# The last layers of a four-layer hybrid network: list-schedule order, and layer norm factors brought to the rows by DMA

## The chip, the cores and the metric

The kernel runs on one core of a Trainium2 chip. The metric is device time in microseconds (us), taken as the median of several runs. A core has five engines with queues of their own: TensorE (PE; its weight loads are listed as PEld), VectorE (DVE), ScalarE (ACT), GpSimd (POOL) and SyncE (SP), which issues the transfers here. Products are written to PSUM, which has eight banks of 2 KB per partition; 512 fp32 columns fill one bank.

## The reference, cut to what matters

Four images of 96 channels and 64x64 pixels pass through four layers. Layers 0 and 1 are state-space scans (Mamba, and a scan in four directions). The change concerns layers 2 and 3, which see each image as 4096 tokens of 96 channels:

```python
t = _to_tokens(x)
t = t + _L2_attn_ref(_ln_t(t), ...)   # spectral: 96->192, BN, ReLU, FFT over 4096 tokens, complex
                                      # diagonal + ReLU, inverse FFT, 192->96, BN
t = t + _L2_ffn_ref(_ln_t(t), ...)    # 96->384->96, operands rounded to fp8e5, sums to fp16
t = t + _L3_attn_ref(_ln_t(t), ...)   # linear attention without softmax, 6 heads of 16
t = t + _L3_ffn_ref(_ln_t(t), ...)    # as the first feed-forward

def _ln_t(v, eps=1e-5):
    m = jnp.mean(v, axis=-1, keepdims=True)
    s = jnp.var(v, axis=-1, keepdims=True)
    return (v - m) / jnp.sqrt(s + eps)
```

There are thus four layer norms over the channels per image: one for the spectral layer, three for the rest. The tokens lie on the free axis and the channels on the partitions, so the mean and the variance of a token are sums over partitions.

## The kernel before

`stage_mamba` and `stage_ss2d` compute layers 0 and 1, and `stage_tokens` computes layers 2 and 3 from the buffer `mid2` in DRAM. The first two stages record every operation in a `Plan`: each operation gets an engine, a modelled cost, its predecessors and, for PSUM tiles of the tag `mm`, a `Hold` on a buffer that is chosen late. `Plan.order` then plays a list schedule over five engine clocks: each engine takes the ready operation with the lowest index, and an operation that finds no free buffer is parked. `Plan.run` issues the operations in that order (in the profile they all stand at L467).

`stage_tokens` is written without the planner: its instructions are issued in the order of the Python code. It works in blocks of W = 512 tokens, eight per image. Two generators run in each round of the loop over images: `spectral(t)` for image b, and the chain `ffn`, `attention`, `ffn` for image b-1 (the rest stream). After each `yield` the loop takes the next step from the stream that has done the smaller share of its steps (`SPECTRAL, REST = 100, 170`). So there are five rounds: image 0's spectral layer alone, three rounds with both streams, and the rest stream of image 3 alone. Inside a stream, `lanes` interleaves two or three blocks with a skew. The spectral stream has four PSUM banks (`pa`), the rest stream three (`pb`), and one more (`pv`) sums the attention's key-value products.

The layer norm (`layer_norm_steps`) does for one block of 512 tokens:

- one product with `center_w` (identity minus 1/96), which gives the centred tokens `ln_cent` in PSUM (L524);
- two passes of ACT: the square to `ln_sq` (L527), and a copy to `d` in SBUF (L528), which is `ln_d` or the output itself;
- four products with `ln_sq` as weights and the column `mean_w` as the moving operand, one column each, which put the variances of 512 tokens into a 128x4 tile `ln_var` (L532);
- `rsqrt`: an add on DVE (L507) and a power on POOL (L509), which give `ln_rs`, 128x4;
- four products (L544) of `ln_rs`, broadcast to 96 columns, with the identity: they bring the factors back to the rows, `ln_rstd`, 96x512 in PSUM;
- one multiply on DVE, `d` times `ln_rstd` (L551 to fp8, L553 to fp32).

The spectral layer computes the 4096-point transform as 64 x 64: `h_ps` (96 to 192 channels, L1442), `fa_ps` (first transform of 64, L1455, two tiles of one bank each, copied out by DVE and ACT), `x_ps` (twiddled second transform, L1470) with `u` on ACT and `z` on DVE, `zw_ps` (L1490), `bz_ps` (L1508) and `o_ps` (L1522). The feed-forward uses `f_ps` (L1539 and L1548) with fp8 operands, with `fy` and `fo` as fp16 steps between and `hq` cast on POOL. The attention uses `kv_ps`, `vk_ps` and `at_ps`. The tile `t` holds an image; there are two, so that image b is loaded once image b-2 has been stored.

## Time and profile before

| | |
|---|---|
| median of 3 runs | 7759.35 us (7758.62 to 7760.86) |
| profiled execution: time | 7736.41 us |
| profiled execution: span of the core | 7734.3 us |
| mean granted TensorE clock | 0.906 |
| PE busy | 6714.1 us (87%) |
| DVE busy | 5775.7 us (75%) |
| POOL busy | 5765.4 us (75%) |
| ACT busy | 4616.8 us (60%) |

The profile is that of one execution, whose own time stands beside its span. Busy time of PE contains records that overlap, since products are pipelined; the granted clock is the share of full speed that the hardware allowed TensorE. In the rows of groups a line number names the place in the kernel, then come engine, operation, output and inputs, shapes, count, busy time and mean duration of one, and the engine's idle time just before, with what ended it. An fp32 product shows as two records.

### The profile page before, as it was taken

What the parts mean: (1) busy time and instruction counts of PE and PEld (TensorE: products, weight loads), DVE (VectorE), ACT (ScalarE), POOL (GpSimd) and SP (SyncE); (2) the same over time, 40 slices, a digit from 0 to 9 for tenths busy, and PEclk for the clock granted to TensorE, in tenths of its full rate; (3) what the DMA queues carried; (4) which work ended last, traced back from release to release, by engine and by line L of the source; (5) the groups of instructions that cost most, each with busy time, mean ns of one, the idle gap of its engine ahead of it and who ended that gap; (6) DMA issues with size and microseconds to landing.
All of it is one profiled execution on the core that took longest, in us unless ns stands there. A gap on an engine that the chain in (4) does not pass through costs nothing.

```text
span 7734.3 us, 84473 instructions
## 1 busy us (share of the span) xinstructions
PE 6714.1 (87%) x28872; PEld 2880.5 (37%) x28872; DVE 5775.7 (75%) x4491; ACT 4616.8 (60%) x6903; POOL 5765.4 (75%) x2836
## 2 busy tenths in 40 slices
PE   7988889888988877879898898889898877999997
PEld 2322233223323222223232322223232226888784
DVE  5989988988898882888888877788888873344343
ACT  4655555555555544767777766677777654445442
POOL 5989988989899882889898978789898971222323
PEclk9999999999999988889999897899899878889897
DMA  6988888988888874888888977788887862000000
GB/s 172 235 231 230 230 212 225 246 221 221 225 230 226 225 190 130 216 214 214 208 217 208 237 185 205 205 205 206 207 211 209 219 170 64 2 17 2 17 9 9
DMA packets 473180, 1374.15 MB, mean 178 GB/s; under 512 B 105678, under 2 KB 123807, under 8 KB 470700
## 3 DMA queue, kind: packets, MB, share of 16 engines
q1 hardware_dynamic: 472748, 1368.76, 68.5%
q8 instruction: 227, 3.72, 0.2%
q14 instruction: 205, 1.68, 0.1%
HBM read 1188.18 MB, written 180.36 MB: 177 GB/s over the span
## 4 chain that ended last, share of the span: by engine, by line
PE 53%; DVE 23%; issue 7%; ACT 6%; POOL 6%; DMA 5%; SPq 0%; DVEq 0%; POOLq 0%; ACTq 0%
PE mm L467 18%; PE s L467 14%; DVE sc_d L467 10%; DVE s L467 6%; PE y L467 5%; DVE sc_u L467 4%; POOL sc_h L467 3%; PE x_ps L1470 2%; DMA sc_d<-dd 2%; PE ln_rstd L544 2%; PE ln_cent L524 2%; PE ln_var L532 2%; PE zw_ps L1490 1%; DVE ysum L467 1%; PE h_ps L1442 1%
## 5 line engine op out<-in xcount | busy, mean ns | idle before, releaser
L467 POOL TENSOR_TENSOR sc_h<-sc_d,bc 128x1024 f32<-128x1024 f32 x1024 | 2407.0, 2357 | 375.5 <-DVE sc_d L467 255.9
L467 DVE TENSOR_TENSOR_SCAN sc_d<-sc_d,carry,s 128x1024 f32<-128x1024 f32 x768 | 1801.2, 2346 | 57.5 <-ACT sc_d L467 7.5
L467 DVE TENSOR_TENSOR s<-s,bc 128x1024 f32<-128x1024 f32 x1024 | 1249.3, 1220 | 503.7 <-PE s L467 339.5
L467 PE MATMUL s<-du,c_sel 96*128 96x512 f32 x2048 | 1170.7, 706 | 245.5 <-DVE sc_d L467 200.3
L467 ACT ACTIVATE sc_d<-sc_d,w_alog 128x1024 f32<-128x1024 f32 x1024 | 1166.8, 1146 | 308.5 <-DMA sc_d<-dd 304.7
L467 POOL TENSOR_TENSOR sc_u<-sc_u,bc 128x1024 f32<-128x1024 f32 x512 | 1207.1, 2358 | 191.8 <-ACT bc L467 117.1
L467 POOL TENSOR_TENSOR sc_h<-sc_u,bc 128x1024 f32<-128x1024 f32 x512 | 1207.2, 2358 | 118.0 <-PE y L467 100.7
L467 PE MATMUL y<-sc_h,c_red 128*32 128x512 f32 x6144 | 1072.4, 650 | 79.1 <-POOL sc_h L467 72.7
L467 DVE TENSOR_TENSOR_SCAN sc_u<-s,carry,sc_u 128x1024 f32<-128x1024 f32 x384 | 895.4, 2332 | 55.3 <-ACT s L467 38.9
L467 PE MATMUL s<-du,c_selp 128*128 128x512 f32 x1408 | 730.6, 648 | 112.4 <-DVE sc_d L467 109.3
L467 PEld LDWEIGHTS s<-du,c_sel 96*128 96x128 f32 x2048 | 419.4, 219 | 915.3 <-issue 464.6
L467 ACT ACTIVATE s<-sc_d,w_alog 128x1024 f32<-128x1024 f32 x512 | 570.6, 1115 | 193.5 <-DVE sc_d L467 117.7
L467 ACT ACT_TABLE_LOAD x492 | 631.2, 1283 | 12.9 <-DMA sc_d<-dd 4.3
L467 DVE TENSOR_TENSOR_SCAN sc_d<-sc_d,s 128x1024 f32<-128x1024 f32 x256 | 583.1, 2283 | 17.7 <-ACT sc_d L467 2.9
L509 POOL TENSOR_TENSOR ln_rs<-ln_rs_e,mhalf 128x4 f32<-128x4 f32 x128 | 134.5, 1052 | 566.7 <-DVE ln_rs_e L507 565.1
L467 PE MATMUL mm<-xp,w_conv 96*96 96x512 f32 x1152 | 523.0, 600 | 4.9 <-ACT bc L467 1.9
L467 PEld LDWEIGHTS y<-sc_h,c_red 128*32 128x32 f32 x6144 | 191.3, 113 | 790.9 <-issue 508.0
L467 PEld LDWEIGHTS s<-du,c_selp 128*128 128x128 f32 x1408 | 262.4, 201 | 540.4 <-issue 269.8
L467 ACT COPY carry<-sc_d 128x1 f32<-128x1 f32 x768 | 142.9, 186 | 478.7 <-DVE sc_d L467 470.2
L467 ACT COPY bc<-mm 128x512 f32<-128x512 f32 x512 | 282.8, 581 | 204.6 <-PE mm L467 199.9
L467 PE MATMUL mm<-hn,conv_w 97*64 97x512 f32 (+1 forms) x1024 | 368.3, 615 | 19.9 <-DVE hn L467 19.8
L467 DVE TENSOR_TENSOR_SCAN sc_u<-s,sc_u 128x1024 f32<-128x1024 f32 x128 | 290.7, 2271 | 25.2 <-ACT s L467 22.4
(211 smaller groups left out, 9436.0 us busy)
## 6 DMA issues: line engine op xcount, KB each, us to landing
sc_d<-dd SPq DMA_DIRECT2D x1536, 512.0 KB
sc_u<-ud SPq DMA_DIRECT2D x512, 512.0 KB
dd<-delta SPq DMA_DIRECT2D x128, 448.0 KB
bc<-bcd SPq DMA_DIRECT2D x64, 512.0 KB
ud<-du SPq DMA_DIRECT2D x192, 128.0 KB
dd<-delta SPq DMA_DIRECT2D x32, 512.0 KB
ud<-du SPq DMA_DIRECT2D x32, 512.0 KB
x<-x0d SPq DMA_DIRECT2D x64, 192.0 KB
```

Source lines behind the costliest of these rows:

```text
L467: getattr(getattr(self.nc, op.engine), method)(*a, **kw)
L509: nc.gpsimd.tensor_tensor(rs, ve, self.mhalf[:p, 0:n], ALU.pow)
L524: nc.tensor.matmul(mps, self.center_w, x[:, cs], start=True, stop=True)
L532: nc.tensor.matmul(vps[:, j:j + 1], sq[:, j * 128:(j + 1) * 128], self.mean_w, start=True, stop=True)
L544: nc.tensor.matmul(rps[:, j * 128:(j + 1) * 128], rs[:, q:q + 1].to_broadcast([128, C]), self.ident, start=True, stop=True,)
L1442: nc.tensor.matmul(ph[q * 64:(q + 1) * 64, j, :], xv[:, g * 4 + j, :], w1t[:, q * C:(q + 1) * C], start=True, stop=True,)
L1470: nc.tensor.matmul(px[:, j, :], fa[q][:, :, g * 4 + j], twid[:, g * 4 + j, :], start=True, stop=True)
L1490: nc.tensor.matmul(pw[:, j, :], zs[q][:, j, :], w2[:, q, :], start=q == 0, stop=q == 1)
```

## The change

`stage_tokens` records its work in a `Plan` too. The order is then the planner's over all images at once; the two streams still decide the index of each operation, with steps weighted by what they hold. Five further edits go with it.

- **The norm.** A local function `norm` replaces `layer_norm_steps` in this stage. The centred tokens stay in PSUM (tag `ln`, four banks) and are read there by the last multiply; the copy to `d` goes. The variance products take every fourth token as weights, so that token 4t+q lands in row t, column q, and run against `mean_w` broadcast to 64 columns; one of the 64 is read. The 128x4 factors are written to a line of 512 numbers in DRAM, and read back to 96 partitions by a second transfer (`rows`); the four products with the identity go.
- **PSUM.** All products share three banks (`mm`), with four for `ln` and one for `vk`.
- **Loads.** Image 0 is loaded before the weights; the weights of the feed-forward use the space of `fa` and are loaded at once instead of by turns through the `kv` buffers; the twiddle table comes in eight pieces.
- **Memory.** The two `xl` tiles with their row of ones are made once; `fo` shares the two buffers of `fy`, and `o` those of `u`.
- **The planner.** An operation may take several buffers of a ring at once (the two `fa_ps` tiles), a freed buffer wakes all parked operations, a product's form includes its type, and `side_by_side` takes the cost of each further product. These also apply to the first two stages, which use the same class.

The loops of `h_ps` and `fa_ps` are the same before and after; each group of products is now one operation of the planner.

```diff
@@ Plan
-            op.form = out.ap[0][1], a[1].ap[0][1]
+            op.form = out.ap[0][1], a[1].ap[0][1], a[2].dtype
...
             if new:
-                assert len(new) == 1
+                assert len({id(h.ring) for h in new}) == 1
                 buffers, parked = free[id(new[0].ring)]
-                if not buffers:
-                    heappush(parked, (op.index, op))
+                if len(buffers) < len(new):
+                    parked.append(op)
                     continue
-                since = min(b[0] for b in buffers)
+                buffers.sort(key=lambda b: b[0])
+                since = buffers[len(new) - 1][0]
...
-                    if parked:
-                        _, o = heappop(parked)
+                    for o in parked:
                         heappush(wait[o.engine], (end, o.index, o))
+                    parked.clear()
@@ stage_tokens
-    nc, tc = k.nc, k.tc
-    k.loose = True
+    tc = k.tc
+    pl = Plan(k.nc, least=180.0)
...
-    pa = ctx.enter_context(tc.tile_pool(name="t_pa", bufs=4, space=PSUM))
-    pb = ctx.enter_context(tc.tile_pool(name="t_pb", bufs=3, space=PSUM))
-    pv = ctx.enter_context(tc.tile_pool(name="t_pv", bufs=1, space=PSUM))
+    dr = pl.pool(ctx.enter_context(tc.tile_pool(name="t_dr", bufs=1, space=DRAM)), 4)
+    ps = pl.pool(
+        ctx.enter_context(tc.tile_pool(name="t_ps", bufs=1, space=PSUM)), 3, {"mm": [128, W], "ln": [C, W]}
+    )
+    nc = k.nc = pl
...
+    ts = [load_image(0)]
...
+    def norm(x, out):
+        cent = ps.tile([C, W], F32, tag="ln", name="ln_cent", bufs=4)
+        nc.tensor.matmul(cent, k.center_w, x, start=True, stop=True)
+        sq = wk.tile([C, W], F32, tag="ln_sq", name="ln_sq", bufs=2)
+        nc.scalar.activation(sq, cent, AF.Square)
+        var = ps.tile([128, 4, 64], F32, tag="mm", name="ln_var")
+        cols = sq.rearrange("p (t q) -> p q t", q=4)
+        with nc.side_by_side(overlap=280.0):
+            for q in range(4):
+                nc.tensor.matmul(
+                    var[:, q, :], cols[:, q, :], k.mean_w.to_broadcast([C, 64]), start=True, stop=True
+                )
+        rs = k.rsqrt(wk, var[:, :, 0], EPS, "ln_rs")
+        rd = dr.tile([1, W], F32, tag="ln_rd", name="ln_rd")
+        nc.sync.dma_start(out=rd.rearrange("o (t q) -> (o t) q", q=4), in_=rs)
+        rows = wk.tile([C, W], F32, tag="ln_rows", name="ln_rows", bufs=3)
+        nc.sync.dma_start(out=rows, in_=bass.AP(rd.tensor, rd.offset, [(0, C), (1, W)]))
+        if out.dtype == F8:
+            nc.vector.tensor_tensor(out, cent, rows, ALU.mult, saturate=False)
+        else:
+            nc.vector.tensor_tensor(out, cent, rows, ALU.mult)
...
-            streams.append((spectral(t), SPECTRAL))
+            if b > 0:
+                ts.append(load_image(b))
+            streams.append((spectral(ts[b], xls[0]), spectral_steps))
...
-            done[n] += 1
-            if next(streams[n][0], streams) is streams:
+            weight = next(streams[n][0], 0)
+            done[n] += weight
+            if not weight:
                 live.remove(n)
+    pl.run(tc)
+    k.nc = pl.nc
```

The planner counts 2.2 us plus a term for the bytes for a transfer (about 3.0 us for `rows`), and for the products the cost of the first plus the given `overlap` for each further one.

## The prediction

> **What bounds the kernel now.** I read the page's slices first, to see where the changed stage lies.

> ```profile
> PE   7988889888988877879898898889898877999997
> POOL 5989988989899882889898978789898971222323
> PEclk9999999999999988889999897899899878889897
> ```

> Each digit is a tenth of busy time in 193 us. Up to slice 33 DVE, POOL and the DMA share the load; from there POOL falls to 2 or 3 and PE stands at 9. That tail, 6411 to 7735 us or 1324 us, is stage_tokens. The earlier stages keep their code, so the answer lies in the tail. Next, the windows over its five rounds: length, then busy us of PE, PEld, DVE, ACT and POOL with instruction counts, granted clock, DMA share, GB/s.

> ```profile
> 6436.00:6468.00 32.00, 26.37 (x144) 18.16 (x144) 6.48 (x16) 8.53 (x16) 8.05 (x8) 0.87 0.29 71
> 6468.00:6620.00 152.00, 139.61 (x2050) 137.00 (x2050) 59.10 (x91) 75.42 (x122) 3.51 (x1) 0.90 0.01 2
> 7220.00:7520.00 300.00, 291.27 (x2868) 243.60 (x2868) 115.02 (x237) 145.36 (x258) 84.59 (x97) 0.93 0.04 12
> 7520.00:7735.00 215.00, 167.20 (x676) 103.20 (x676) 63.59 (x133) 64.09 (x120) 72.02 (x89) 0.74 0.03 9
> ```

> Image 0's norms take 32 us and its spectral layer, alone, 152 us. Then come three rounds of 300 us with both streams, PE 97% busy. The last round holds the rest stream alone: PE 78% busy at clock 0.74. No other engine is above 50%, so TensorE bounds the stage: its work, its clock, and its waits at the seams. Third, the groups (busy us, mean ns; idle before). An fp32 product is two records.

> ```profile
> L544 PE MATMUL ln_rstd<-c_ident,ln_rs 128*96 128x128 f32 x1024 | 173.7, 320 | 34.4 <-POOL ln_rs L509 34.4
> L524 PE MATMUL ln_cent<-t,c_center 96*96 96x512 f32 x256 | 158.6, 707 | 24.6 <-DMA t<-mid 20.3 <-DVE t L1528 4.3
> L532 PE MATMUL ln_var<-c_mean,ln_sq 96*128 96x1 f32 x1024 | 139.4, 257 | 13.6 <-ACT ln_d L528 9.4 <-ACT ln_sq L527 4.1
> L1522 PE MATMUL o_ps<-c_twid,bz 128*96 128x64 f32 x512 | 87.6, 342 | 0.7 <-ACT bz L1513 0.7
> ```

> The 128 layer norms (8 + 24 per image) take 472 us of PE busy time. Records overlap, so the true price is start to start, from the timeline: a full-clock stretch of a mixed round, then the last round.

> ```profile
> 7126.11 0.98 PE L532 MATMUL ln_var<-c_mean,ln_sq 96*128 96x1 f32 x8
> 7126.94 2.90 PE L1470 MATMUL x_ps<-c_twid,fa 128*96 128x128 f32 x16
> ...
> 7131.44 1.04 PE L544 MATMUL ln_rstd<-c_ident,ln_rs 128*96 128x128 f32 x8
> 7132.32 2.83 PE L1470 MATMUL x_ps<-c_twid,fa 128*96 128x128 f32 x16
> ...
> 7135.20 1.02 PE L524 MATMUL ln_cent<-t,c_center 96*96 96x512 f32 x2
> 7136.06 0.38 PE L1539 MATMUL f_ps<-xq,f 96*128 96x512 fp8e5 x1
> ```

> ```profile
> 7565.26 2.02 PE L544 MATMUL ln_rstd<-c_ident,ln_rs 128*96 128x128 f32 x8 [0.46 <-POOL ln_rs L509]
> 7567.07 1.06 PE L1548 MATMUL f_ps<-hq,f 128*96 128x512 fp8e5 x2
> ...
> 7574.02 2.02 PE L544 MATMUL ln_rstd<-c_ident,ln_rs 128*96 128x128 f32 x8 [0.71 <-POOL ln_rs L509]
> ```

> At full clock a norm costs PE 0.83 us (variance), 0.88 (rstd) and 0.86 (centring); in the last round rstd alone costs 1.81 plus a 0.46 us wait, in a block of 8.76 us. Last, the chain across the stage's start (start, us).

> ```profile
> 6402.65 2.68 DMA szt<-szd
> 6417.26 5.10 DMA f_in<-in_w_f_dram
> 6425.42 10.87 DMA t<-mid
> 6436.29 1.99 PE ln_cent L524 x2
> ```

> The image is loaded behind all the weights, and PE waits for it until 6436.

> **The change, part by part.** *rstd products.* Removed: 512 products. In a mixed round 32 norms x 0.88 = 28 us at full clock (by busy time 40; the rest is overlap). In the last round, 16 feed-forward norms x (1.81 + 0.46) = 36, and 8 attention norms, at clock near 1, x 0.88 = 7.

> *Variances in 64 columns, from strided weights.* Not in the trace. Lower bound: the single-column price, 0.83. Upper: o_ps, also 64 columns with strided weights, eight records in 2.52 / 2 = 1.26 us (16 records in 2.52 us in the chain). I take the middle, 1.05, since the old one is already paced by weight loading: +0.22 x 32 = 7 us a round (0 to 14), some 8 in the last round at its lower clock (0 to 20).

> *Factors through DRAM.* Added per norm: a write of 2 KB, then a read of 192 KB to 96 partitions. The read has a row, szt<-szd, 2.68 us. For the write the nearest rows are SP's waits for bcd<-bc_part, 196.2 us in 105 waits, longest 5.8; I take 2.7 (2 to 5.8). Norm latency: 0.86 + 0.60 (square) + 1.05 + 0.16 + 1.05 (pow) + 2.7 + 2.68 + 0.68 (multiply) + 8 handoffs of 0.1 = 10.6 us, all with the centred tokens in PSUM. Four such banks give one norm per 2.65 us: 85 us for the 32 norms of a round, under its 300; 64 for the last round's 24, under its 215. I cost it at nothing there: x_ps, zw_ps and the others cover it in mixed rounds. Without cover it shows where norms come in a row ahead of other work, at the start (below). On DVE the multiply now waits for a DMA, and z, fy and the fa copies are queued behind it. The planner counts 2.2 and 3.0 us for the two transfers, so it is placed in time if these hold; a write of 5.8 would be 3 us late, 96 us a round out of the 185 that DVE idles. On SP, 256 more issues of 0.43 us, 110 us in 1324, with a wait of 2.7 us before each read; image loads and stores queue behind it, but SP now waits 1276 us for POOL at L1555.

> The trace has PE at clock 0.67 in 10 us windows of the last round although PE is 85% busy there, and at 1.00 in windows as busy with x_ps. [...]

> *ACT and POOL.* 128 copies to ln_d or xl go (0.577 us each, 74 us of ACT), and with them 9.4 us of PE waits; six of eight memsets (3.5 us) leave POOL. Off the path otherwise.

> *List order and banks.* Seven PSUM banks for products (four spectral, three rest) become three shared ones, plus four for centred tokens. Gains: rounds are no longer walled off, so work fills seams such as 7216 to 7246, at clock 0.50 to 0.82. Full-clock PE work of a mixed round now: spectral 140 (152 less waits in fa), norms 32 x 2.57 = 82, feed-forward 96 products x 0.22 = 21, attention 27 (kv, vk and at, 123.6 / 4 less overlap): 270, against 300 measured; 24 of the 30 are the clock (0.92), the rest waits. After: 270 - 28 + 7 = 249. I keep 27 of the 30: seams fill, three banks add waits. Round 276, minus 24; three rounds, minus 72.

> *Last round.* -43 + 8, and list order recovers 10 of PE's 48 idle us: minus 45. The next limits are lower: POOL per block 1.05 + 3 x 0.61 + 1.16 = 4.1 us; the two fy buffers, now also holding fo, 3.9 us; PE 6.5.

> *Start.* The image is issued first. All of 6.2 MB at the 312 GB/s seen there take 20 us from 6413; the factors queue behind c_twid, so the first multiply comes near 6437, the last four norms a bank turn (10.6) later, h near 6450 instead of 6468: minus 15 (0 to -25). Image 0's own 152 us stay.

> *Earlier stages.* The planner wakes all parked steps instead of one and adds the type to a form. Their only bf16 product has 48 rows, a form of its own already. Zero, bounds 10 either way.

> *What is nothing.* The loops of the first transform (fa) stand in the same order as before; its two tiles are taken together.

> Sum: -72 - 45 - 15 = -132 us on the profiled execution's 7736.4, so 7604. The median, 7759.35, is 23 above that execution; I carry that over: **7627 us**.

> **Rivals.** *A, the waits at the seams go as well.* Mixed rounds at 249 + 12 = 261 (minus 39 each), the last one at full clock, minus 75, start -20: -212, 7547. For it: x_ps stretches already run at 1.00. Against: norms alone do not.

> *B, three banks take back the gain of the mixed rounds.* Losses of 50 instead of 27 give 299; 60 are left from start and end: 7700.

> *C, three banks make it slower.* Per round some 230 tiles pass through them. Product plus evacuation: x_ps 32 x 3.2 = 102, zw 41, h 34, fa 43, bz 21, o 27, f 74, kv 20, at 13, var 39: 414 us, and 46 for two handoffs each: 460. In a 276 us round three banks offer 828, 56% used. The place: fa takes two banks at once, while single-bank steps grab each one that comes free, and ACT and DVE, half busy, keep tiles waiting. It decides once holds exceed 2.1 times these sums (980 / 3 = 327 us a round eats the other 60 and 16 more); at 2.3 times, 353 us a round: +153 - 60, 7852. For it: the old streams had seven banks. Against: in 6510 to 6580 x_ps and zw_ps kept PE 99% busy on four banks with no other stream.

> *D, no change,* where losses near 70 a round just cancel it: 7759.

> **How the numbers follow.** Chances: forecast 0.55, A 0.12, B 0.13, C 0.15, D 0.05. A measurement of this kernel can tell 0.2%, 15.5 us, from no change. Forecast, A and B are faster: 0.80; D same: 0.05; C slower: 0.15. The forecast's own range is 7575 to 7695, from the start (15), variances (40), the last round (25), early stages (10) and 15 us of loss per round, not all at once. The whole range, 7540 to 7770, leaves out C and the lower part of A.

> **What would show it.** Right: no L544 rows in the tail; PE busy in the tail down by 100 to 150 us; var rows between 140 and 215 us; mixed rounds of 270 to 285 us, the last near 170; h_ps starting 15 us earlier after the weights. Wrong: waits of PE for ACT or DVE to free mm tiles above 30 us a round (B, C); waits for DMA rows ahead of xq or h_ps, and a last round that stays above 200; or stages before 6411 that move by more than 10 us.

## The result, and the profile after

The changed kernel takes 7781.19 us (median of 16 runs, 7764.6 to 7813.15), the kernel before 7759.67 us (16 runs). The ratio is 1.003, with an interval of 1.0018 to 1.0042. It is slower by 21.5 us, where 7627 us and a gain were predicted, and the time lies above the range (7540 to 7770).

The profiled execution after took 7785.78 us, its span is 7783.6 us. Against the profile of before that is 49 us more, of which 20 lie ahead of the changed stage. The last addition of the scan stage ended at 6434.0 us (before: 6413.8); among all the kernels below it ended anywhere from 6399 to 6445 us. I therefore compare the tail from that moment on: 1320.5 us before, 1349.7 after, 29 more. These are single executions: planner_only, whose last stage is that of before, has a tail of 1333.8 us, so some 13 us of the 29 can be chance, most of it in the start. First, the same lines of the page as before:

```profile
PE   7988888888988877889898888889898877999997
POOL 5989989988898972889898969689898871221313
PEclk9999999999999988889898898889898877789786
```

PE is as busy in the tail as before, but the granted clock in the last seven slices fell from 8889897 to 7789786. Next, the windows by round of the kernel after: length, then busy us of PE, PEld, DVE, ACT and POOL with counts, granted clock, DMA share and GB/s. A round ends with the last addition of an image's spectral output; the first line holds image 0's norms and its spectral layer.

```profile
6434.00:6656.80 222.80, 178.96 (x2152) 165.40 (x2152) 73.44 (x123) 82.69 (x136) 14.66 (x13) 0.76 0.18 49
6656.80:6959.10 302.30, 295.93 (x2587) 238.12 (x2587) 115.64 (x225) 126.20 (x218) 71.01 (x85) 0.84 0.12 26
6959.10:7270.20 311.10, 305.37 (x2614) 242.72 (x2613) 124.65 (x238) 130.52 (x227) 80.32 (x96) 0.82 0.14 32
7270.20:7581.20 311.00, 304.02 (x2606) 242.25 (x2606) 125.39 (x238) 128.93 (x224) 79.16 (x95) 0.82 0.13 29
7581.20:7783.60 202.40, 158.39 (x499) 95.47 (x497) 71.46 (x142) 57.64 (x105) 79.96 (x98) 0.67 0.16 36
```

In a mixed round PE has 250 to 280 matmuls fewer than before, and yet it is busy 296 to 305 us instead of 289 to 295. So in these rounds PE does not wait more; its instructions take longer. The same cuts for the kernels that matter below (us, with the granted clock in brackets; one profiled execution each):

| kernel | start and image 0 | mixed 1 | mixed 2 | mixed 3 | last | tail |
|---|---|---|---|---|---|---|
| before | 206.9 (0.85) | 295.4 (0.92) | 303.7 (0.92) | 300.4 (0.93) | 214.1 (0.74) | 1320.5 |
| planner_only | 215.0 (0.79) | 295.9 (0.93) | 305.1 (0.91) | 303.8 (0.92) | 214.1 (0.74) | 1333.8 |
| after | 222.9 (0.76) | 302.3 (0.84) | 311.2 (0.82) | 310.9 (0.82) | 202.4 (0.67) | 1349.7 |
| contig_weights | 214.8 (0.79) | 278.0 (0.88) | 301.3 (0.80) | 293.6 (0.83) | 199.0 (0.65) | 1286.7 |
| no_round_trip | 190.7 (0.84) | 299.2 (0.83) | 307.7 (0.83) | 307.2 (0.83) | 182.2 (0.69) | 1287.0 |
| wide_strided | 215.0 (0.82) | 293.9 (0.91) | 306.9 (0.88) | 305.9 (0.86) | 204.4 (0.71) | 1326.2 |
| before_wide | 205.9 (0.86) | 285.0 (0.97) | 291.6 (0.96) | 290.9 (0.96) | 206.0 (0.84) | 1279.4 |
| wide_contig | 208.2 (0.85) | 268.6 (0.91) | 272.8 (0.94) | 280.1 (0.92) | 197.4 (0.73) | 1227.1 |
| list_old_norm | 190.7 (0.89) | 285.2 (0.92) | 286.8 (0.94) | 282.3 (0.96) | 167.1 (0.84) | 1212.1 |
| wide_old_norm | 189.1 (0.90) | 276.3 (0.98) | 281.1 (0.98) | 280.7 (0.99) | 153.1 (0.91) | 1180.3 |
| wide_no_round_trip | 182.1 (0.90) | 254.3 (0.97) | 263.1 (0.97) | 259.0 (1.00) | 169.3 (0.80) | 1127.8 |

before and planner_only run the same last stage: their rounds agree within 3.4 us, but for the start, which differs by 8.

**The variance products.** The groups of the kernel after in the tail, the variances and the centring (busy us, mean ns; idle before):

```profile
L472 PE MATMUL mm<-c_mean,ln_sq 96*128 96x64 f32 x1024 | 256.8, 413 | 31.0 <-ACT ln_sq L472 30.5 <-ACT fa L472 0.4
L472 PE MATMUL ln<-t,c_center 96*96 96x512 f32 x256 | 193.5, 854 | 31.9 <-DVE xl L472 18.7 <-DMA t<-mid 11.0 <-DVE t L472 2.1
```

The variances are busy 256.8 us instead of 139.4, and a record lasts 413 ns instead of 257. Start to start, from the timeline of a stretch where the clock still stood at 1.00:

```profile
6869.01 1.02 PE L472 MATMUL ln<-t,c_center 96*96 96x512 f32 x2
6869.87 1.43 PE L472 MATMUL mm<-c_twid,fa 128*96 128x128 f32 x8
6871.14 1.98 PE L472 MATMUL mm<-c_mean,ln_sq 96*128 96x64 f32 x8
6872.95 1.99 PE L472 MATMUL mm<-w_w,z 96*128 96x96 f32 x16
```

The centring still takes 0.86 us, the variances of one norm 1.81 (6871.14 to 6872.95) instead of 0.83. That is 0.98 us more, and the products with the identity that went away had cost 0.88. Over the whole tail it is the same: the 57 norms whose variances ran at full clock (0.98 or more) and had no wait behind them have a median of 1.85 us (before: 0.81 of 89). On PE the change is thus a loss before anything else counts.

**The start.** The timeline of PE after the image has come:

```profile
6452.55 3.87 PE L472 MATMUL mm<-c_mean,ln_sq 96*128 96x64 f32 x16
6473.37 3.73 PE L472 MATMUL ln<-t,c_center 96*96 96x512 f32 x4 [16.95 <-DVE xl L472]
6476.89 3.79 PE L472 MATMUL mm<-c_mean,ln_sq 96*128 96x64 f32 x16
...
6495.48 4.77 PE L472 MATMUL mm<-w1t,xl 97*64 97x96 f32 x58 [7.74 <-DVE xl L472]
```

After four norms the four banks of centred tokens are full, and PE waits 17 us for the first multiply, then 7.7 us for the last ones; `h_ps` (the last line) begins 61 us after the scan stage's end, where it was 54 before. The timeline of SP and DVE shows what the multiply waited for:

```profile
6458.71 1.62 SPq L472 DMA_DIRECT2D ln_rd<-ln_rs  x2
6469.64 0.79 SPq L472 DMA_DIRECT2D ln_rows<-ln_rd  x2
6472.62 0.69 DVE L472 TENSOR_TENSOR xl<-ln,ln_rows 96x512 f32<-96x512 f32 x1 [15.94 <-DMA ln_rows<-ln_rd]
```

The 2 KB write was issued at 6458.7, behind the loads of the twiddle table and behind four more, those of image 1, and the read could only follow at 6469.6:

```profile
6447.73 5.31 SPq L472 DMA_DIRECT2D c_twid<-in_c_twid_dram  x8
6453.24 4.49 SPq L472 DMA_DIRECT2D t<-mid  x4
```

In the last round, where no load is ahead of it, the two took 2.3 and 3.9 us (write issued at 7598.01, read at 7600.28, multiply at 7604.14):

```profile
7598.01 0.34 SPq L472 DMA_DIRECT2D ln_rd<-ln_rs  x1
7600.28 0.38 SPq L472 DMA_DIRECT2D ln_rows<-ln_rd  x1
7604.14 0.69 DVE L472 TENSOR_TENSOR xq<-ln,ln_rows 96x512 fp8e5<-96x512 f32 x1 [2.37 <-DMA ln_rows<-ln_rd]
```

**The clock.** One stretch of the kernel after, as a window: 44 us in which PE is never idle and yet has the clock 0.50 throughout.

```profile
6929.10:6973.50 44.40, 44.40 (x175) 33.54 (x173) 18.28 (x28) 15.13 (x26) 14.97 (x18) 0.50 0.22 55
```

| work in a piece of 3.41 us | ten kernels: pieces, share followed by clock 1.00 | last four: pieces, share |
|---|---|---|
| under 2000 | 590, 0.00 | 94, 0.00 |
| 2000 to 2250 | 220, 0.04 | 28, 0.04 |
| 2250 to 2500 | 237, 0.18 | 32, 0.28 |
| 2500 to 2750 | 265, 0.50 | 52, 0.56 |
| 2750 to 3000 | 216, 0.74 | 52, 0.73 |
| over 3000 | 2220, 0.99 | 1090, 1.00 |

A piece at half clock also does less work, so the table alone could be read the wrong way round. Split by the clock of the piece itself, the steps stay: over all fourteen tails the shares for the six rows are 0.00, 0.02, 0.21, 0.58, 0.70 and 0.98 behind pieces at half clock, and 0.00, 0.00, 0.22, 0.64, 0.83 and 1.00 behind pieces at full clock. The count holds for this stage; in the stages ahead of it 12% of the 3286 pieces under 2000 were followed by full clock.

In the 44 us above the work of the pieces is some 1750 to 2450, most of them below 2400. The time that PE is busy says far less: of the pieces of the kernel after that have PE busy over 95% at half clock, 29 of 108 are followed by full clock.

By this count, which is an estimate, one norm of before gave 1152 (centring: 2 records x 512 x 2 x 0.75 x 0.75), 12 (variances) and 1536 (identity products: 8 x 128 x 2 x 0.75): 2700 in 2.57 us at full clock, or 3590 a piece. One norm of after gives 1152 and 768 (8 x 64 x 2 x 0.75): 1920 in 0.86 + 1.81 = 2.67 us, or 2450 a piece, on the edge. At half clock (1.71 + 1.80 us) it gives 1870, and would never get the clock back by itself. Centring alone, at half clock without a gap, gives 2300.

### The profile page after: what moved, and what is told of

It reads as the page before. It is cut to its first block, busy times and chain, and to the rows that moved or that the text cites. A ratio compares the mean times of both kernels' runs of the same rounds, so it can differ in the third digit from the quotient of the medians.

```text
span 7783.6 us, 82958 instructions
## 1 busy us (share of the span) xinstructions
PE 6783.5 (87%) x27848; PEld 2883.1 (37%) x27848; DVE 5803.9 (75%) x4491; ACT 4563.6 (59%) x6775; POOL 5741.9 (74%) x2830
## 3 DMA queue, kind: packets, MB, share of 16 engines
q14 instruction: 209, 1.71, 0.1%
## 4 chain that ended last, share of the span: by engine, by line
PE 31%; DVE 10%; ACT 4%; issue 4%; DMA 3%; POOL 3%; SPq 0%; POOLq 0%; DVEq 0%; ACTq 0%
PE mm L472 20%; PE s L472 7%; DVE sc_d L472 4%; DVE s L472 3%; PE y L472 2%; PE ln L472 2%; POOL sc_h L472 1%; DVE sc_u L472 1%; DVE ysum L472 1%; DMA bc_in<-dd 1%; ACT bc L472 1%; DMA sc_d<-dd 1%; ACT L472 1%; ACT s L472 1%; ACT delta L472 0%
## 5 line engine op out<-in xcount | busy, mean ns | idle before, releaser
L472 PE MATMUL s<-du,c_sel 96*128 96x512 f32 x2048 | 1183.1, 712 | 218.3 <-DVE sc_d L472 181.0
L472 POOL TENSOR_TENSOR ln_rs<-ln_rs_e,mhalf 128x4 f32<-128x4 f32 (+1 forms) x224 | 247.1, 1103 | 836.9 <-DVE ln_rs_e L472 776.6
L472 PEld LDWEIGHTS mm<-c_mean,ln_sq 96*128 96x128 f32 x2048 | 393.7, 269 | 210.0 <-ACT ln_sq L472 89.8
L472 PE MATMUL mm<-c_mean,ln_sq 96*128 96x1 f32 (+1 forms) x2048 | 400.4, 337 | 63.8 <-ACT ln_sq L472 37.0
```

The source lines that it names most:

```text
L472: getattr(getattr(self.nc, op.engine), method)(*a, **kw)
```

## The experiments

The theory after the result: (1) weights taken as every fourth element make the variance products slow; (2) without the identity products the norms no longer earn the full clock; (3) the round trip shows where no other stream covers it. The rivals: the planner's edits disturb the earlier stages; three banks starve PE (rival C of the prediction); the list order itself is worse. Every ratio is to the kernel before, timed beside the experiment, with its 95% interval; the medians of before there were 7752.6 to 7764.8 us, so differences of a few us between two experiments are not clear.

### planner_only: the planner's edits alone

The kernel before, with the new `Plan` in the first two stages.

```diff
-                if not buffers:
-                    heappush(parked, (op.index, op))
+                if len(buffers) < len(new):
+                    parked.append(op)
...
-                    if parked:
-                        _, o = heappop(parked)
+                    for o in parked:
                         heappush(wait[o.engine], (end, o.index, o))
+                    parked.clear()
```

> The kernel before with nothing but the planner's edits (all parked steps woken, the type in a form, several buffers at once); its last stage is untouched. Theory P (the planner's edits lengthen the scan stage: its last residual add came at 6430.7 us in the changed kernel's profile and at 6413.2 in that of before): the last add moves to about 6430, time +12 to +20 us, ratio 1.002. Theory W (the loss is all in the variance products of the last stage): the last add within 5 us of 6413 once several executions are looked at, ratio 0.999 to 1.001.

Measured: 7764.21 us, ratio 1.0001 (0.9987 to 1.0015). The planner's edits cost nothing that can be measured. This execution's scan stage ended at 6430.6 us, 17 later than in the profile of before. In before_wide below, whose scan stages are those of before, it ended at 6445.4: so the shift ahead of the tail differs from execution to execution, and the change need not explain it.

### contig_weights: the same products from contiguous weights

ACT writes the squares in the order that the products take them, so that their weights are contiguous; 64 columns remain.

```diff
-        nc.scalar.activation(sq, cent, AF.Square)
+        nc.scalar.activation(
+            sq.rearrange("p (q t) -> p t q", q=4), cent.rearrange("p (t q) -> p t q", q=4), AF.Square
+        )
...
-        cols = sq.rearrange("p (t q) -> p q t", q=4)
+        cols = sq.rearrange("p (q t) -> p q t", q=4)
```

> The changed kernel, but ACT writes the squares in the order in which the variance products read them, so that their weights lie side by side (64 columns kept; the square costs ACT about 0.45 us more). Theory W (weights read every fourth element set the price of a variance norm, 1.81 us start to start on PE at full clock where 0.83 was paid before, and the idle array lowers the clock): the price falls to 0.8 to 1.0, the four mixed and last rounds by 25 to 35 us each, clock in the mixed rounds up from 0.82 to 0.9 or more, time 7640 to 7680. Theory R (the round trip through DRAM holds PE up and cools it): price falls but the rounds by under 10 us and the clock stays below 0.85, time 7740 to 7780.

Measured: 7729.6 us, ratio 0.9962 (0.9944 to 0.998), 52 us less than after. The group and, from the timeline at full clock, one norm:

```profile
L472 PE MATMUL mm<-c_mean,ln_sq 96*128 96x64 f32 x1024 | 181.0, 338 | 38.5 <-ACT ln_sq L472 36.5 <-ACT fa L472 1.2 <-DVE fa L472 0.2
```

```profile
6868.98 1.00 PE L472 MATMUL mm<-c_mean,ln_sq 96*128 96x64 f32 x8
```

The eight records take 1.00 us instead of 1.98. The mean of 338 ns is still above the 257 of before, because much of the tail runs at half clock (1.76 us a norm there, 6964.00 to 6965.76 in the timeline). Part (1) is shown, and without it the kernel is faster than before; but the clock of the mixed rounds (0.80 to 0.88) did not reach the expected 0.9, and most of the expected gain is still missing.

### strided_one_column: the strided weights with one column

```diff
-        var = ps.tile([128, 4, 64], F32, tag="mm", name="ln_var")
+        var = ps.tile([128, 4], F32, tag="mm", name="ln_var")
...
-                    var[:, q, :], cols[:, q, :], k.mean_w.to_broadcast([C, 64]), start=True, stop=True
+                    var[:, q:q + 1], cols[:, q, :], k.mean_w, start=True, stop=True
```

> The changed kernel with one column per variance product in place of 64, weights still every fourth element. Theory W: the price is that of the load, so it stays near 1.8 us a norm and the time within 15 us of 7781. Rival, columns (64 columns instead of one cost the time): price back to 0.8 to 1.0, time 7650 to 7690.

Measured: 7812.38 us, ratio 1.0074 (1.0054 to 1.0094): 31 us slower than after, though it streams one column instead of 64. Two things follow. The price is that of loading the weights: the weight loads of the tail last 328 ns each, as in after, and at full clock the variances of a norm take 1.80 us start to start with one column (median of 49 norms) and 1.85 with 64. And the 63 idle columns were worth something: the loss was expected to stay within 15 us of after. The mixed rounds grew to 315, 327 and 317 us at clocks of 0.77 to 0.79: that was the first sign that the clock goes by work and not by busy time.

### no_round_trip: the factors not fetched

The multiply reads a constant tile in place of the fetched factors.

```diff
-        rd = dr.tile([1, W], F32, tag="ln_rd", name="ln_rd")
-        nc.sync.dma_start(out=rd.rearrange("o (t q) -> (o t) q", q=4), in_=rs)
-        rows = wk.tile([C, W], F32, tag="ln_rows", name="ln_rows", bufs=3)
-        nc.sync.dma_start(out=rows, in_=bass.AP(rd.tensor, rd.offset, [(0, C), (1, W)]))
+        rows = ones
```

> The changed kernel without the two transfers of the factors: the multiply reads a tile of ones, so the tokens are centred but not scaled. Variances, add and power are kept. Theory R: mixed rounds fall from 311 to 280 us or below and the last from 204 to 160, time 7650 or less. Theory W: variance products stay at 1.8 us, mixed rounds stay above 295; the start gains 15 to 20 us and the last round 10 to 30, time 7720 to 7750.

Measured: 7709.02 us, ratio 0.9938 (0.9919 to 0.9957), 72 us less than after. The windows of the start with image 0, of the first mixed round and of the last:

```profile
6445.10:6635.80 190.70, 173.33 (x2152) 160.26 (x2152) 73.45 (x130) 82.80 (x136) 14.76 (x13) 0.84 0.16 47
6635.80:6935.00 299.20, 297.12 (x2585) 239.26 (x2585) 121.19 (x228) 126.85 (x218) 73.01 (x87) 0.83 0.03 9
...
7549.90:7732.10 182.20, 149.81 (x493) 91.83 (x493) 71.62 (x138) 55.49 (x101) 77.35 (x95) 0.69 0.04 11
```

The start is 32 us shorter and the last round 20; each mixed round 3 to 4. The clock of the start rose from 0.76 to 0.84, but that of the mixed rounds stays at 0.83 (after: 0.82 to 0.84) and that of the last round at 0.69 (0.67). So in these rounds the waits for transfers are not what holds the clock down.

### wide_contig, wide_strided, before_wide: array work added

If the clock goes by work, useless work should make a kernel faster. The centring gets 128 output rows (`center128` is `center_w` with 32 of its columns copied behind it) and the variances 128 columns; what is added is never read.

```diff
-        cent = ps.tile([C, W], F32, tag="ln", name="ln_cent", bufs=4)
-        nc.tensor.matmul(cent, k.center_w, x, start=True, stop=True)
+        wide = ps.tile([128, W], F32, tag="ln", name="ln_cent", bufs=4)
+        nc.tensor.matmul(wide, k.center128, x, start=True, stop=True)
+        cent = wide[0:C, :]
...
-                    var[:, q, :], cols[:, q, :], k.mean_w.to_broadcast([C, 64]), start=True, stop=True
+                    var[:, q, :], cols[:, q, :], k.mean_w.to_broadcast([C, 128]), start=True, stop=True
```

wide_contig has both on top of contig_weights; wide_strided has both on after; before_wide has both in the last stage of before.

> contig_weights with two paddings that add array work and no PE time at full clock: 128 identical columns in a variance product in place of 64, and a centring product with 128 output rows in place of 96 (32 rows are copies that nothing reads). Theory H (the clock of a 3.41 us window is granted by the array work of the window before: streamed columns x passes x rows/128 x output rows/128, threshold near 2500; a feed-forward block of the last round brings 2403 per window at half clock with 64 columns and 96 rows, and so stays there however busy PE is; padded it brings over 3000): clock 0.95 or more in the mixed rounds, rounds near 265 us, the last from 199 to 165 or less, time 7600 to 7640. Rival R (PE cools because it waits for the factors): the clock stays at 0.80 to 0.88 and the time within 15 us of contig_weights, 7715 to 7745.

> The changed kernel with the same two paddings, weights still every fourth element. Theory H: clock in the mixed rounds from 0.82 to 0.95, rounds from 311 to 280, the last from 202 to 175, time 7650 to 7690. If the strided loads alone cost the time (theory W without the clock): no change, 7770 to 7790.

> The kernel before with the two paddings in its last stage (one column to 128 in a variance product, contiguous weights as they were; centring to 128 rows). PE does not get less to do. Theory H: mixed rounds from 300 to 275-285 us, the last from 214 to 160-180, clock there from 0.74 to 0.95, time 7630 to 7690. Rival (the clock follows PE's busy time or its gaps): no gain, 7755 to 7775.

Measured: wide_contig 7654.59 us, ratio 0.9865 (0.9851 to 0.988), 75 us less than contig_weights; wide_strided 7756.67 us, 0.9996 (0.9984 to 1.0007), 25 us less than after; before_wide 7705.38 us, 0.993 (0.9914 to 0.9946), 55 us less than before. The variances and the centring of wide_contig, and its mixed rounds:

```profile
L472 PE MATMUL mm<-c_mean,ln_sq 96*128 96x128 f32 x1024 | 165.2, 311 | 54.5 <-ACT ln_sq L472 52.4 <-ACT fa L472 1.2
L472 PE MATMUL ln<-t,center 96*128 96x512 f32 x256 | 154.3, 695 | 40.7 <-DVE xl L472 25.5 <-DMA t<-mid 10.5 <-DVE xq L472 2.6
```

```profile
6632.20:6900.80 268.60, 257.43 (x2579) 210.39 (x2580) 116.43 (x223) 139.27 (x215) 70.11 (x84) 0.91 0.14 29
6900.80:7173.60 272.80, 259.50 (x2614) 211.80 (x2613) 123.47 (x238) 145.65 (x226) 80.38 (x96) 0.94 0.18 36
7173.60:7453.60 280.00, 265.07 (x2616) 212.84 (x2615) 123.32 (x238) 145.77 (x227) 80.38 (x96) 0.92 0.15 33
```

Twice the columns are busy for less time (165.2 us against 181.0), and a third more output rows of centring too (154.3 against 190.8). The clock of the mixed rounds rose from 0.80 to 0.88 up to 0.91 to 0.94. These mixed rounds lie where the prediction had put them (270 to 285 us).

All three runs gained, and all three less than expected: the last rounds stayed at 197, 204 and 206 us, and wide_strided's mixed rounds fell by no more than 4 to 8 us though their clock rose to 0.86 to 0.91. So part (2), that the array's work holds the clock up, is shown. What it is worth depends on the weights: the added work brings 25 us with strided weights and 75 with contiguous ones, and contiguous weights bring 52 us without the added work and 102 with it, 127 us for both together. The kernel before gains 55 us by it too: its clock was short of work already (0.92 and 0.93 in the mixed rounds, 0.96 and 0.97 with the added work).

### four_banks: the rival C

```diff
-        ctx.enter_context(tc.tile_pool(name="t_ps", bufs=1, space=PSUM)), 3, {"mm": [128, W], "ln": [C, W]}
+        ctx.enter_context(tc.tile_pool(name="t_ps", bufs=1, space=PSUM)), 4, {"mm": [128, W], "ln": [C, W]}
...
-        cent = ps.tile([C, W], F32, tag="ln", name="ln_cent", bufs=4)
+        cent = ps.tile([C, W], F32, tag="ln", name="ln_cent", bufs=3)
```

> The changed kernel with four shared product banks in place of three, and three for centred tokens in place of four. Theory of the banks (three are too few): mixed rounds fall by 10 us or more each, time 7750 or less. Theories W and H: mixed rounds within 5 us of 311, the last round up to 5 us longer, time 7770 to 7795.

Measured: 7801.6 us, ratio 1.0059 (1.004 to 1.0078). Together the fourth bank for products and the bank less for the centred tokens make the kernel 20 us slower, and two of the mixed rounds grew from 311 to 326 and 328 us, where 5 us had been allowed. The run does not separate the two banks; PE's waits for `xl` ahead of a centring product, which the bank less would explain, grew from 18.7 to 32.6 us in the tail. What a fourth bank for products could give is seen in PE's waits in the kernel after, over the whole tail (total, times, longest):

```profile
PE mm L472 <- ACT fa L472: 7.4, 13, 0.7
...
PE mm L472 <- ACT fy L472: 2.1, 3, 0.7
PE mm L472 <- DVE z L472: 1.8, 4, 0.6
```

These are the waits that a product tile not yet freed could explain, 11.3 us in 1350; with the fourth bank they come to 1.8 us. Rival C is out.

### list_old_norm: the list order with the norm of before

Order, banks, loads and memory of after; in `norm` one column and contiguous weights, the copy on ACT and the four identity products of before.

```diff
+        nc.scalar.copy(d, cent)
+        var = ps.tile([128, 4], F32, tag="mm", name="ln_var")
+        cols = sq.rearrange("p (q t) -> p q t", q=4)
...
+        rows = ps.tile([C, W], F32, tag="mm", name="ln_rstd")
...
+                    rows[:, j * 128:(j + 1) * 128], rs[:, j:j + 1].to_broadcast([128, C]), k.ident,
```

> List order, banks and loads of the changed kernel with the norm of the kernel before: contiguous weights, one column, 96 rows, a copy of the centred tokens to SBUF, and the factors brought to the rows by four products. Theory H: PE has the work of before and the rstd products carry array work (three quarters of the array, 128 columns), so the clock in the mixed rounds is 0.88 to 0.95 and the rounds 285 to 300 us; the start is that of before within 10 us; time 7710 to 7760. Rival (the list order with shared banks is itself the loss): rounds above 305, time above 7775.

Measured: 7635.9 us, ratio 0.9844 (0.9829 to 0.9858). Its windows by round:

```profile
6424.30:6614.90 190.60, 172.11 (x2232) 161.23 (x2232) 73.48 (x123) 87.49 (x146) 14.67 (x13) 0.89 0.16 47
6614.90:6900.10 285.20, 284.08 (x2831) 240.25 (x2832) 116.18 (x228) 141.75 (x251) 73.83 (x88) 0.92 0.03 10
...
7469.20:7636.30 167.10, 138.70 (x685) 91.82 (x685) 69.39 (x139) 66.09 (x125) 76.47 (x94) 0.84 0.04 13
```

The list order, with the banks, loads and memory that came with it, gains 117 us by the medians, even with three banks (7710 us had been expected at best), and in the first mixed round PE is busy 284 of 285 us. The edits of the norm (strided weights, factors by transfer, identity products gone) then lose 145 us. This splits the change in two parts of opposite sign, and it settles the rival that the list order is worse. The clock shows part (2) from the other side: the mixed rounds have 0.92 to 0.96 here, and 0.80 to 0.88 in contig_weights, which has contiguous weights too but no identity products.

### wide_old_norm: the same with the array work added

```diff
-        nc.tensor.matmul(wide[0:C, :], k.center_w, x, start=True, stop=True)
+        nc.tensor.matmul(wide, k.center128, x, start=True, stop=True)
...
-                    var[:, q:q + 1], cols[:, q, :], k.mean_w, start=True, stop=True
+                    var[:, q, :], cols[:, q, :], k.mean_w.to_broadcast([C, 128]), start=True, stop=True
```

> list_old_norm with the two paddings of wide_contig (128 columns, 128 rows). It is wide_contig with the factors brought by products instead of two transfers. Theory H with the round trip priced at the start and in the last round only: mixed rounds 10 to 20 us longer than wide_contig's 274, clock 0.95; the start 8 to 15 us shorter than its 208; the last round 160 to 180 where it had 197; time 7640 to 7670. If the transfers are the better way everywhere: 7680 or more.

Measured: 7597.63 us, ratio 0.9796 (0.978 to 0.9812). It is 2% faster than before, better than the 7640 to 7670 us expected, and beats both kernels; only wide_no_round_trip, which goes without the factors, takes less. The second mixed round and the last, from the windows:

```profile
6864.20:7145.30 281.10, 279.67 (x2869) 238.27 (x2869) 121.62 (x238) 145.45 (x258) 79.57 (x96) 0.98 0.04 13
...
7426.00:7579.10 153.10, 126.05 (x681) 84.73 (x681) 67.07 (x136) 64.91 (x123) 75.65 (x93) 0.91 0.05 14
```

Against wide_contig, which fetches the factors through DRAM, it is 57 us faster by the medians: even with contiguous weights and the clock restored, four products per norm are cheaper than the two transfers. They are so at the two ends alone: its start is 19 us shorter and its last round 44, while its mixed rounds are up to 8 us longer.

### wide_no_round_trip and late_twiddles: where the transfers still cost

wide_no_round_trip is wide_contig with the edit of no_round_trip (`rows = ones`). late_twiddles is wide_contig with the twiddle table loaded behind image 0's last norm:

```diff
-    for g in range(8):
-        nc.sync.dma_start(out=twid[:, g * 8:(g + 1) * 8, :], in_=k.w["c_twid"][:, g * 8:(g + 1) * 8, :])
...
+        if t is ts[0]:
+            for g in range(8):
+                nc.vector.tensor_copy(twid[0:C, g * 8, 0:1], xl[0:C, (NW - 1) * W:(NW - 1) * W + 1])
+                nc.sync.dma_start(out=twid[:, g * 8:(g + 1) * 8, :], in_=k.w["c_twid"][:, g * 8:(g + 1) * 8, :])
```

> wide_contig without the two transfers; the multiply reads a tile of ones, so tokens are centred but not scaled. What is left of the price of the round trip once the clock is up: start 15 to 25 us shorter, the last round from 197 to 160, mixed rounds 0 to 10 shorter each; time 7580 to 7610. If the last round is bound by PE and not by the trip: 197 stays within 10, time 7620 to 7640.

> wide_contig with the 4 MB of c_twid loaded only once image 0's last norm is through (a one-element copy ahead of each piece holds it back), so that the first factors do not queue behind it. First products (x_ps) need it some 40 us later. Expected: the first multiply about 12 us earlier after the stage's start, start 208 to about 195 us, all else equal, time 7640 to 7650. If the queue behind c_twid is not what delays the first factors: within 5 us of 7655.

Measured: wide_no_round_trip 7552.41 us, ratio 0.9737 (0.972 to 0.9755), 102 us less than wide_contig. Its rounds are 182, 254, 263, 259 and 169 us: 26 less at the start, 10 to 21 in each mixed round (0 to 10 were expected), 28 in the last. late_twiddles took 7640.28 us, 0.9851 (0.9836 to 0.9867): 14 us less than wide_contig, though the two intervals overlap, and its start is 201 us where it is 208 in wide_contig and 182 without transfers. So the queue behind the table is a part of the loss at the start, 7 of 26 us. The rest is not the round trip alone: image 1's loads are still ahead of the first write, which is issued at 6429.78 and lets its read follow only at 6437.99. No run takes these loads away.

## Why the prediction was wrong, step by step

**The price of the variance products** is the first term that failed. The prediction took its upper bound of 1.26 us from the rows of `o_ps`, as 64 columns with strided weights, and allowed 0 to 14 us a round. Measured: 1.81 us, +0.98 x 32 = 31 us a round. The profile of before already held the hint. The products of `o_ps` load 96 weight columns and take 0.315 us for a product of two records; by an estimate per weight column, 128 columns make 0.42 us a product and 1.68 us a norm. The bound was taken from a row without scaling it by what was loaded, on an operation that the text itself said was paced by its weight loads. At clock 1.00, eight records take 1.98 us strided (after) and 1.00 contiguous (contig_weights) with the same 64 columns; no run shows why the stride costs that.

**The clock** was in the sum as a constant: of the 30 us that a mixed round of before lost, 24 of them by its clock of 0.92, the prediction kept 27, whatever the change took from PE. And it counted the full-clock price of the identity products (0.88) as a gain. That price came out somewhat lower: at clocks near 1, the mixed rounds of wide_old_norm are 22, 18 and 22 us longer than those of wide_no_round_trip, against 28 predicted. But by the count above these products carried more than half of a norm's array work, and without them the norms fell to the edge of what holds the clock here (2450 a piece, by the same estimate). The prediction saw the 0.67 at 85% busy in the last round, and 1.00 in windows as busy with `x_ps`, and still gave its sum no term for a change of the clock. Busy time does not explain the clock here: PE was 100% busy for 44 us at half clock, and idle columns and output rows made a kernel faster (before_wide, 55 us). Nor do the waits for transfers explain it in the last round, which saved 12 us of the 45 counted: its clock was 0.67, and with the transfers gone it still was 0.69 (no_round_trip). A mixed round can be put together so: 300 before, -15 by the list order (list_old_norm), -21 to -28 for the identity products, +31 for the variances, makes 288 to 295. Measured were 302 to 311. The rest, some 15 us, goes with the clock (0.82 to 0.84, where list_old_norm has 0.92 to 0.96); that split is worked out, not measured by itself, and wide_strided, whose clock is 0.86 to 0.91, gets back 4 to 8 us of it.

**The round trip at the start** was the right mechanism with the wrong size. The prediction had the factors queue behind the table and the bank turn of the last four norms, and put the first multiply 24 us after the scan stage's end, `h_ps` 36 and the start at -15 us. Loading the image first did what was expected: PE had it 7 us after that end (before: 22). But the first multiply came after 39 us, since the write waited 11 us behind the table and image 1's loads and then took as long to land, the last norms another 23 later, `h_ps` after 61, and the start is +16 (of which 8 can be chance). Without the transfers `h_ps` begins after 36.5 us (no_round_trip), and with the old norm the start is indeed -16 (190.7).

**The round trip in the last round** was costed at nothing, by 64 us of throughput under 215 of round. It costs 20 us (no_round_trip). A bound by throughput says nothing of a chain: one norm in the last round waits 6.1 us for its two transfers, and with one stream there is not always other work.

**The round trip in the mixed rounds** was rightly costed at nothing for this kernel (3 to 4 us a round). But that holds while PE is slow enough to cover it: in wide_contig, with the clock back, it is 10 to 21 us a round.

**The last round's 45 us** came from the wrong edit. The prediction gave 43 to the identity products and 10 to the list order. The list order with its banks, loads and memory brings 214 to 167 with those products in place; the norm's edits bring it back to 202.

**What was right:** the planner's edits cost nothing; three banks do not hold PE up; rival C had the sign of the result but not its mechanism (and by its own 353 us a round its price is +159, not +153); the list order with its other edits gains more than was allowed (15 us a mixed round where 3 were kept), 5 to 8 us of it PE's idle time. Of the marks that the prediction set, the identity products are gone, but PE's busy time in the tail rose by 33 us instead of falling by 100, the variances stand at 256.8 us, above the 215, and the last round at 202, above the 200 that would show it wrong.

What stays open: why the clock goes with this work (rows, output rows and columns fit; no run separates rows from output rows), and the share of the clock in each round, since the strided loads slow PE (1.98 us instead of 1.00 for eight records) and lower its work at once.

## What to carry to other kernels

A product that looks removable may be what keeps the TensorE clock up: with the identity products the mixed rounds have 0.92 to 0.96 (list_old_norm), without them 0.80 to 0.88 (contig_weights). As far as this stage shows, count the array work that each 3.41 us still holds (columns x steps x rows x output rows; 99% of the pieces over 3000 were followed by full clock, under 1% of those under 2000) ahead of counting busy time, and try idle columns or output rows where it falls short (25 to 75 us here). Price a product with few columns by the weights that it loads (strided, a norm takes 1.80 us with one column and 1.85 with 64) and by how they lie in memory (eight records take 1.98 us strided, 1.00 contiguous), scaled from a row that loads as many. A round trip through DRAM was nearly free here only where a chain, and not just the throughput, had other work beside it: 3 to 4 us in a mixed round, 20 in the last and 32 at the start (no_round_trip); look first at the place where one stream runs alone.

## What was not expected of the hardware

- The variance products from every fourth element take 1.85 us a norm at full clock (median of 57 norms) and 1.87 at half clock (40 norms), where the centring takes 1.71 us at half clock and 0.86 at full: the price of these products hardly depends on the clock.
- In this stage the clock of the next 3.41 us goes with the array work of this one, with the change between 2250 and 3000: in ten kernels full clock followed 18% of the pieces of 2250 to 2500 and 74% of those of 2750 to 3000.
- While POOL cleared the two rows of ones, small operations of DVE that otherwise take 0.15 us lasted over 3 us, and ended when a memset did (the memsets ended at 6433.92 and 6437.41, the operations at 6433.95 to 6433.96 and 6437.44). The scan stage's last addition (the third line) is one of them, 3.30 us instead of 0.68, so 2.6 of the 20 us ahead of the tail go with the changed stage's own memsets:

```profile
6430.39 3.56 DVE L472 TENSOR_SCALAR bn_rs_e<-w_v 96x2 f32<-96x2 f32 x2 [2.28 <-PE mm L472]
6430.42 6.99 POOL L472 MEMSET xl<- 1x4096 f32 x2 [1.22 <-PE mm L472]
6430.66 3.30 DVE L472 TENSOR_TENSOR x<-x,mm 96x512 f32<-96x512 f32 x1
6434.09 3.35 DVE L472 CAST fb<-fb2q 96x2 f32<-96x2 fp8e5 x1
```
